# Local-attention and whitening kernel: the first image prepared as a whole, the row point at infinity by column points in images 2 and 3, interpolations one bank later

## The chip, the cores and the metric

The kernel runs on one NeuronCore of a Trainium2 chip, with everything in float32. The metric is device microseconds (us) of one launch. A core has five engines with a queue each: TensorE (PE, matmuls and transposes through the array; its weight loads are shown apart as PEld), VectorE (DVE), ScalarE (ACT), GpSimd (POOL) and SyncE (SP, which here only issues DMAs). Each engine takes its own instructions in order and waits on semaphores for the others.

## The reference, cut to what matters

```python
k = lax.conv_general_dilated(x, w1, padding=[(6, 6), (6, 6)], rhs_dilation=(2, 2), ...) + b1   # 7x7, 256 -> 128 channels
k = lax.conv_general_dilated(k, w2, ...) + b2                                                   # 1x1, 128 -> 49
attn = jax.nn.softmax(k, axis=1)
shifts = jnp.stack([xp[:, :, 2*u:2*u+64, 2*v:2*v+64] for u in range(7) for v in range(7)], axis=1)
y = jnp.einsum('bkchw,bkhw->bchw', shifts, attn)
# then, over all images: 4 groups of 64 channels, covariance Sigma, five Newton steps P = 1.5 P - 0.5 P^3 Sigma_N, and wm (y - mean)
```

The input x has 4 images (numbered 0 to 3 here) of 256 channels by 64 by 64 pixels.

## The kernel before, in words

**Layout.** The two convolutions are multiplied into one, 256 to 49 channels, 7 by 7 taps. A dilation of 2 splits an image into even and odd rows, and each of these into even and odd columns. One half of the rows goes to output partitions 0 to 48, the other to 64 to 112, so a result tile has 113 partitions.

**The convolution by points.** Along each axis the sum of 7 taps is a product of polynomials, and both factors are evaluated at seven points: 0, 1, -1, 2, -2, 1/2 and infinity (`INF`, number 6). A *row point* is handled in these steps. `row_eval` (L423) evaluates x along the rows into one of three tiles `rb`. `col_eval` (L454) evaluates that along the columns into seven tiles `xh`, in three *banks*: points (1, 2, 0), (3, 4, 6) and (5). `weights` (L355) makes, the first time that a row point is met, the weights of a bank by the same kind of sums, and stores them in DRAM (`gd`); later images load them from there. `conv_bank` (L482) multiplies a bank on TensorE into one of two PSUM tiles `cv`, and ScalarE copies it to `pv`. When the three banks are done, `col_interp` (L556) interpolates the seven column points back to columns, and writes row `br` of the tile `zz`. When all row points of an image are there, `row_interp` (L569) interpolates along the rows and gives the logits. Both call `interpolate` (L517), a chain of 22 VectorE operations that is written out in an order by hand, on elements of 113x162 (columns) or 113x576 (rows). Its work tile is `it`, a piece of the tile `ct`, for columns (`ct` is also the scratch of `col_eval` and `weights`), and a tile of its own, `zi`, for rows.

**Direct rows.** A row point can also be convolved without column points, with the 7 column taps as they stand (`direct`, L594: 28 products of up to 512 columns). Image 0 does row points 1, 2, 3 by column points and INF, 0, 4, 5 directly; images 1 to 3 do 0 to 5 by column points and INF directly (`direct_inf`, L632).

**Image 0** (L698 to L756) is a list written by hand, and `in_turn` (L277) makes VectorE keep exactly that order. In it, the interpolation of row 1 stands between the preparations of rows 3 and 5, and that of row 2 behind row 5.

**Images 1 to 3** run as 18 *steps* each, `conv_step` (L655) for six row points by three banks: multiply a bank; prepare the same bank of the next row point in the same tiles (`xh` and the weight tiles have one buffer); after the third bank, interpolate. The last two row points are interpolated `in_order` (L292), at high priority. Between the steps lie *gaps*, set by costs (6, 5, 2 for the banks of a row, 12 for the direct row; L1146 to L1164): gap j of an image comes when (j+1)/8 of the cost is done. Into the gaps `plan` (L1109) has put the softmax of the image before (`soft`), and the attention: `first_half` and `second_half` of four pixel classes n per image. These load bands of attention weights from DRAM (`band`), turn them by VectorE transposes (`load_band`, L890), transpose x and multiply (`weighted_sum`), transpose the result and add up the moments. TensorE keeps the program's order; the other engines' queues are ordered by a planner, by priority and its own costs.

**Loads.** GpSimd's queue fetches images 1 to 3; image 2's and 3's halves go into space that the attention of an earlier image must have left (`move`, L1021). SP's queue has all the other DMAs, each waiting its turn.

After image 3's convolution the remaining attention runs alone (about 605 to 695 us), then whitening, then the application to all pixels (to 765 us).

Of the kernel before, what the change touches and what calls it, by code (L numbers as in the profile page):

```python
# [27 lines left out]
ROWS = (0, 1, 2, 3, 4, 5)  # L28
# [3 lines left out]
def kernel(  # L32
# [222 lines left out]
    zz = apool.tile([P, NP - 1, Q9, W], F32, name="zz")  # L255
    zi = [apool.tile([P, Q9, W], F32, name=f"zi{k}") for k in range(2)]
    for k in range(2):
        nc.gpsimd.memset(zi[k], 0.0)
    ct = apool.tile([P, Q8 * 4 * Q8, 4], F32, name="ct")
    it = ct.rearrange("p a b -> p (a b)")[:, :PT].rearrange("p (q b) -> p q b", q=Q9)  # L260
# [10 lines left out]
    gd = [dram.tile([P, nsl, NSK], F32, name=f"gd{b}") for b in range(NP - 1)]  # L271
# [42 lines left out]

    def keep_weights(br):
        f = (gb5 if br == 5 else gbr).rearrange("p v a r k -> p (v a r k)")
        nc.scalar.mul(f, f, SCALE[br])
        nc.sync.dma_start(kept[br], f)

    def row_weights(br):  # L320
# [8 lines left out]
        if br == 1:  # L329
            add(E, T[6], T[4])  # L330
            add(O, T[5], T[3])
            add(S0, E, O)
            add(E1, T[2], T[0])
# [4 lines left out]
        elif br == 3:  # L338
            madd(E, T[4], 4.0, T[6])
            madd(O, T[3], 4.0, T[5])  # L340
            madd(S0, O, 2.0, E)
            madd(E1, T[0], 4.0, T[2])
            madd(S1, T[1], 2.0, E1)
        elif br == 4:
            madd(S0, O, -2.0, E)
            madd(S1, T[1], -2.0, E1)
        else:
            madd(S0, T[6], 2.0, T[5])
            madd(S0, S0, 2.0, T[4])
            madd(S0, S0, 2.0, T[3])  # L350
            madd(S1, T[2], 4.0, T[0])
            madd(S1, T[1], 2.0, S1)
            add(S1, S1, S1)

    def weights(b, br, i):  # L355
# [9 lines left out]
        wt = apool.tile([P, ns, NSK], F32, tag=f"wr{i}", name=f"wr_{b}_{br}_{i}")  # L365
# [7 lines left out]
        elif br in kept:  # L373

            f = rb[0].rearrange("p q r c w -> p (q r c w)")[:, : KS * NSK]
            if i == 0:
                nc.sync.dma_start(f, kept[br])
            f = f.rearrange("p (v a r k) -> p v a r k", v=KS, a=NCC, r=2)
            g = [f[:, v] for v in range(KS)]
        else:  # L380
            g = [gbr[:, v] for v in range(KS)]
        g = [t.rearrange("p a r k -> p (a r k)") for t in g]
        e, o, e1 = (
            ct.rearrange("p a b -> p (a b)")[:, k * NSK : (k + 1) * NSK] for k in range(3)
        )
# [4 lines left out]
        if i == 0:  # L390
            add(e, g0[0], g0[2])
            add(o, g0[1], g0[3])
            add(o0[1], e, o)
            sub(o0[2], e, o)
            add(e1, g1[0], g1[2])
# [4 lines left out]
        elif i == 1:  # L400
            madd(e, g0[2], 4.0, g0[0])
            madd(o, g0[3], 4.0, g0[1])
            madd(o0[3], o, 2.0, e)
            madd(o0[4], o, -2.0, e)
            madd(e1, g1[2], 4.0, g1[0])
# [3 lines left out]
        else:  # L409
            madd(o0[5], g0[0], 2.0, g0[1])  # L410
            madd(o0[5], o0[5], 2.0, g0[2])
            madd(o0[5], o0[5], 2.0, g0[3])
            madd(o1[5], g1[0], 4.0, g1[2])
            madd(o1[5], g1[1], 2.0, o1[5])
# [8 lines left out]
    def row_eval(b, br, rb=rb):  # L423

        for pr in range(2):
# [5 lines left out]
            elif br == 0:  # L431
                nc.scalar.copy(r[2], xs[:, 0])
            for cc in range(NCC):
                X = [xs[:, a, :, cc] for a in range(4)]
                q = [t[:, :, cc] for t in r]
                if br == 3:
                    madd(q[1], X[2], 4.0, X[0])
                    madd(q[2], X[3], 4.0, X[1])
                elif br == 5:
                    madd(q[2], X[0], 2.0, X[1])  # L440
                    madd(q[2], q[2], 2.0, X[2])
                    madd(q[2], q[2], 2.0, X[3])
# [9 lines left out]
        return rb[{1: 2, 2: 0, 3: 0, 4: 1, 5: 2, 0: 2}[br]]  # L452

    def col_eval(src, i):  # L454
# [9 lines left out]
        if i == 0:  # L464
            add(EO, X[:, :, 0:2], X[:, :, 2:4])
            add(o[1], E, O)
            sub(o[2], E, O)
            nc.scalar.copy(o[0], X4[0])
        elif i == 1:
            madd(EO, X[:, :, 2:4], 4.0, X[:, :, 0:2])  # L470
            madd(o[3], O, 2.0, E)
            madd(o[4], O, -2.0, E)
            nc.scalar.copy(o[INF], X4[3])
        else:
            madd(o[5], X4[0], 2.0, X4[1])
            madd(o[5], o[5], 2.0, X4[2])
            madd(o[5], o[5], 2.0, X4[3])

    ncv = [0]
    pvs = {}  # L480

    def conv_bank(b, br, i, w):  # L482

        if i == 0:
            pvs[b, br] = apool.tile(
                [P, NP, Q9, 2 * Q9], F32, tag="pv", name=f"pv_{b}_{br}", bufs=2
            )
# [23 lines left out]
        with tc.high_priority():  # L511
            nc.scalar.copy(  # L512
                pvs[b, br][:K2, i0 : i0 + len(pts)].rearrange("p n q b -> p (n q b)"),
                cv[:K2, : len(pts)].rearrange("p n q b two -> p (n q b two)"),
            )

    def interpolate(pt, tmp, outs, cut, part=None):  # L517

# [8 lines left out]
        if part != 1:  # L527
# [4 lines left out]
            add(s3, c0, c6)  # L532
            sub(s3, tmp, s3)
            madd(s1, tmp, -2.0, s1)
            madd(tmp, tmp, -30.5, s1)
            madd(tmp, s3, 22.5, tmp)
            madd(s1, c0, 1.5, s1)
            madd(s1, c6, -30.0, s1)
            madd(s3, s1, -1.0 / 6, s3)
            sub(s4, s4, s2)  # L540
            madd(tmp, s2, -16.0, tmp)
            add(tmp, tmp, s4)
            madd(outs[0], lo(s1), 1.0 / 6, hi(c0))
            add(outs[2], lo(c6), hi(s3))
        if part != 0:
            madd(hh, tmp, -1.0 / 9, hh)
# [5 lines left out]
    def phases(t):  # L552

        return [t[:, :, bass.ds(4 + a - R if a < R else 0, Q8, 4)] for a in range(4)]

    def col_interp(b, br, part=None):  # L556
        pv = pvs[b, br]
        pt = {c: pv[:K2, i] for i, c in enumerate(ORDER)}
        outs = phases(zz[:K2, br].rearrange("p q (w two) -> p q w two", two=2))
        cut = lambda t, k: t[:, :, 2 * k : 2 * (k + Q8)].rearrange("p q (b two) -> p q b two", two=2)  # L560
        t = it
        if part is not None:

            t = pvs[b, ROWS[-2]][:, 0]
        interpolate(pt, t[:K2], outs, cut, part)
# [818 lines left out]
```

## Time and profile before

| | |
|---|---|
| median of 3 runs | 761.5 us (761.24 to 763.82) |
| the profiled execution: its time | 767.1 us |
| its span, first to last instruction | 765.3 us |
| PE busy, of the span | 710.7 us, 93% |
| DVE busy | 630.3 us, 82% |
| ACT busy | 332.4 us, 43% |
| image 0's convolution | to about 171 us |
| images 1, 2, 3 (from one direct row to the next) | about 171 to 301, 301 to 453, 453 to 605 us |

How to read it: busy time is the union of an engine's instructions. A matmul's end is modelled, so a busy PE isn't PE at its peak; and consecutive VectorE instructions overlap in the records, so what one costs is read from the distance between two starts, not from its own duration. Times in the text count from the span's start.

### The profile page before, as it was taken

The page shows a single profiled execution, that of the slowest core. Times are in us where ns is not written, and L with a number is a line of the kernel's source. Part 1 is how long each engine was busy: PE and PEld are TensorE (multiplying, and loading weights), DVE is VectorE, ACT ScalarE, POOL GpSimd, SP SyncE. Part 2 cuts the span into 40 slices and gives each one's busy share as a digit, 9 for nine tenths or more (in the row PEclk, how much of TensorE's full clock was granted, in tenths as well). Part 3 has the DMA queues.
Part 4 walks back from the last instruction along what each step waited for, and adds up shares of the span by engine and source line. Part 5 has one row for each costly group of instructions (what it writes and reads, how often), then busy time and mean ns, then how long its engine had stood idle before and what let it go on. Part 6 is the DMA issues. An engine that isn't in the chain of part 4 may idle for free.

```text
span 765.3 us, 18542 instructions
## 1 busy us (share of the span) xinstructions
PE 710.7 (93%) x7512; PEld 538.0 (70%) x7512; DVE 630.3 (82%) x1312; ACT 332.4 (43%) x958; POOL 34.4 (4%) x48
## 2 busy tenths in 40 slices
PE   6989899969899999989999999999999889998996
PEld 1449564365798887779988967798898768885322
DVE  3769999999899999989996899699979775645565
ACT  2413241025555454366444443635435473322464
POOL 0410000020000010001000100000000000000000
PEclk9999999979999999999999999999999999999999
DMA  8991110042654393056734920533532233362487
GB/s 323 238 322 65 39 75 38 1 155 68 200 153 156 122 351 91 20 160 205 235 120 141 313 70 1 155 90 110 166 88 80 49 115 128 115 251 111 190 362 327
DMA packets 59773, 114.76 MB, mean 150 GB/s; under 512 B 22903, under 2 KB 42024, under 8 KB 58920
## 3 DMA queue, kind: packets, MB, share of 16 engines
q1 hardware_dynamic: 55992, 94.71, 37.5%
q0 software_dynamic: 3696, 18.88, 7.2%
q8 instruction: 59, 0.97, 0.5%
q14 instruction: 26, 0.21, 0.1%
HBM read 66.23 MB, written 47.33 MB: 148 GB/s over the span
## 4 chain that ended last, share of the span: by engine, by line
DVE 43%; PE 32%; ACT 5%; issue 5%; DMA 2%; SPq 0%; DVEq 0%; ACTq 0%
PE y L955 10%; PE cv L502 7%; DVE xh L307 5%; PE tp L1324 4%; DVE rb L307 3%; DVE pv L307 3%; DVE zz L307 3%; DVE ct L307 3%; DVE ct L300 3%; DVE band L908 3%; PE sig L1008 3%; PE tp L987 2%; PE tp L926 2%; DVE pv L303 2%; DVE rb L300 2%
## 5 line engine op out<-in xcount | busy, mean ns | idle before, releaser
L502 PE MATMUL cv<-xh,wr 128*49 128x128 f32 x4368 | 253.7, 278 | 14.3 <-DVE xh L300 11.5
L502 PEld LDWEIGHTS cv<-xh,wr 128*49 128x49 f32 x4368 | 247.3, 125 | 19.9 <-issue 12.9
L955 PE MATMUL y<-band,xb 128*128 128x224 f32 (+2 forms) x640 | 153.4, 379 | 12.5 <-ACT xb L934 8.3
L955 PEld LDWEIGHTS y<-band,xb 128*128 128x128 f32 x640 | 111.2, 196 | 34.4 <-ACT xb L934 10.8
L974 ACT ACTIVATE slot<-y,pivot 128x512 f32<-128x512 f32 x53 | 36.7, 740 | 60.0 <-PE y L955 60.0
L512 ACT COPY pv<-cv 113x486 f32<-113x486 f32 (+1 forms) x63 | 29.8, 474 | 74.9 <-PE cv L502 73.7
L995 ACT COPY yt<-tp 128x256 f32<-128x256 f32 x128 | 45.5, 379 | 34.8 <-PE tp L987 33.8
L926 PE MATMUL tp<-ident,slot 128*128 128x128 f32 x256 | 50.3, 299 | 7.1 <-ACT yt L995 7.1
L987 PE MATMUL tp<-ident,slot 128*128 128x128 f32 x256 | 52.0, 299 | 4.0 <-ACT xb L934 1.4
L908 DVE STREAM_TRANSPOSE band<-band 128x960 f32<-128x960 f32 (+1 forms) x48 | 50.8, 1059 | 4.9 <-DMA band<-sd 4.8
L987 PEld LDWEIGHTS tp<-ident,slot 128*128 128x128 f32 x256 | 41.3, 205 | 13.9 <-issue 4.5
L926 PEld LDWEIGHTS tp<-ident,slot 128*128 128x128 f32 x256 | 40.0, 206 | 14.4 <-ACT yt L995 9.0
L857 ACT COPY zt<-d 32x112 f32<-32x112 f32 (+2 forms) x156 | 45.0, 288 | 1.7
L811 ACT ACTIVATE d<-tp,mx 128x49 f32<-128x49 f32 x128 | 37.0, 336 | 15.1 <-DVE mx L806 15.1
L307 DVE SCALAR_TENSOR_TENSOR xh<-ct 128x512 f32<-128x512 f32 x42 | 27.7, 681 | 12.2 <-PE cv L502 12.0
L934 ACT COPY xb<-tp 128x256 f32<-128x256 f32 x87 | 30.4, 376 | 15.8 <-PE tp L926 15.2
L1008 PE MATMUL sig<-yt 128*64 128x65 f32 x1024 | 36.9, 225 | 0.0
L1008 PEld LDWEIGHTS sig<-yt 128*64 128x64 f32 x1024 | 32.5, 138 | 6.0 <-issue 4.4
L608 PE MATMUL cv<-slot,wi 128*49 128x496 f32 (+3 forms) x168 | 34.8, 571 | 0.0
L934 DVE COPY xb<-tp 128x256 f32<-128x256 f32 x41 | 16.4, 421 | 22.2 <-PE tp L926 22.2
L307 DVE SCALAR_TENSOR_TENSOR pv<-pv 113x162 f32<-113x162 f32 x105 | 33.5, 319 | 1.0
L419 ACT ACTIVATE wr<-wr 128x392 f32<-128x392 f32 (+1 forms) x36 | 17.3, 512 | 31.1 <-DVE wr L300 18.8
(224 smaller groups left out, 999.9 us busy)
## 6 DMA issues: line engine op xcount, KB each, us to landing
out_dram<-out SPq DMA_DIRECT2D x32, 512.0 KB, 3.4
sd<-zt SPq DMA_DIRECT2D x16, 896.0 KB, 3.9
slot<-in_x_dram POOLq DMA_DIRECT2D x12, 1024.0 KB, 9.6
band<-sd SPq DMA_DIRECT2D x128, 84.0 KB, 2.1
wr<-gd SPq DMA_DIRECT2D x15, 588.0 KB, 3.8
wr<-gd SPq DMA_DIRECT2D x15, 490.0 KB, 3.6
spill<-slot POOLq DMA_DIRECT2D x3, 2048.0 KB, 8.4
back<-spill SPq DMA_DIRECT2D x3, 2048.0 KB, 7.7
```

The lines of the kernel that those rows point to most:

```text
L300: return in_turn(TT(o, a, b, ALU.add))
L307: return in_turn(STT(o, a, f, b, ALU.mult, ALU.add))
L502: nc.tensor.matmul(cv[h * HB : h * HB + KT, k, sr : sr + n, sc : sc + n], wv[:, sc, sr, cc], xh[bc][:, :n, h * NCC + cc, :n], start=(j == ...
L811: nc.scalar.activation(d[:, h, i], lt[i // NI][:, i % NI, h, :KT], AF.Exp, bias=mx[:, i, h : h + 1], accum_out=s[:, h, i : i + 1],)
L857: ins = nc.scalar.copy(o, i)
L908: nc.vector.transpose(f, f)
L926: nc.tensor.transpose(t[:, cc * P : (cc + 1) * P], xt[:, cc, CR * m : CR * (m + 1), bass.ds(pc, SW, 2)], ident,)
L934: (nc.vector.tensor_copy if tail else nc.scalar.copy)(xb, t[:, :C])
L955: nc.tensor.matmul(ps[:, cc, q0 - half * HALF : q1 - half * HALF, :], xb[:, cc * P : (cc + 1) * P], rhs, start=(k == 0), stop=(k == len(PI ...
L987: nc.tensor.transpose(t[:, cc * P : (cc + 1) * P], yt[:, cc, CR * i : CR * (i + 1), bass.ds(pc, SW, 2)], ident,)
L995: nc.scalar.copy(yb.rearrange("p a g c -> p (a g) c")[:, :, :GW], t[:, :C].rearrange("p (e c) -> p e c", c=GW),)
L1008: nc.tensor.matmul(sig[g * GW : (g + 1) * GW, cc], yb[:, cc, g, :GW], yb[:, cc, g], start=(count[0] == 0 and cc == 0), stop=(count[0] == 4 ...
```

## The change

It has these parts.

- **Order of operations.** In `interpolate`, `weights`, `row_weights` and `row_eval` the same VectorE operations come in another order, in which fewer of them touch what the one just before them wrote or read. For image 0, `both0` deals the operations of `weights` and `col_eval` of a bank out alternately (so `weights` has its scratch in slot 4 there, not in `ct`); `col_ops` is `col_eval` as a generator that pauses behind its first operation.
- **Image 0's list.** All rows are evaluated and multiplied first, and the three column interpolations come behind `row_eval(0, 5)`.
- **INF by column points.** `ROWS` begins with INF. Images 2 and 3 have seven row points and no direct row. Image 1's direct INF is done at the end of image 0's list, with the taps that still lie in SBUF, and not in its steps. INF's weights are made in image 2 (half as long as the others, 98 elements) and loaded in image 3. `zz` gets a seventh row; `zi` and the tile `wi` are gone.
- **Interpolation one bank later.** A row's `col_interp` is issued behind the preparation that follows the *next* row's first bank. `pv` has three slots, not two, and `col_interp`'s work tile is a piece of a `pv` slot, not of `ct`; `row_interp`'s is now in `ct`. ScalarE's last copy of an interpolation is ordered behind the next second bank (`later`).
- **Steps and gaps.** Softmax (0, 0) comes before image 1's first bank and softmax (0, 1) behind its third. INF's steps cost half, so that the gaps shift against the rows: in image 1 gap 2 comes behind row 2's first bank (before: row 1's second), gap 5 behind row 4's second (before: its first); in images 2 and 3 gap 0 comes behind row 0's first bank, with INF's three banks ahead of it.
- **First transposes.** For n = 0 the three band transposes are kept in a list, `held`, and ordered behind the last operation of softmax (0, 1).

```diff
-ROWS = (0, 1, 2, 3, 4, 5)
+ROWS = (INF, 0, 1, 2, 3, 4, 5)
...
+    NV = 3
+    pv = apool.tile([P, NV, NP, Q9, 2 * Q9], F32, name="pv")
...
+    kept[INF] = dram.tile([P, KS * NSK // 2], F32, name="gi")
+    nc.sync.dma_start(kept[INF], tap[:, UPOS[3]].rearrange("p v a k -> p (v a k)"))
...
@@ weights @@
         if i == 0:
             add(e, g0[0], g0[2])
             add(o, g0[1], g0[3])
+            add(e1, g1[0], g1[2])
             add(o0[1], e, o)
             sub(o0[2], e, o)
-            add(e1, g1[0], g1[2])
...
             madd(o0[5], g0[0], 2.0, g0[1])
+            madd(o1[5], g1[0], 4.0, g1[2])
             madd(o0[5], o0[5], 2.0, g0[2])
+            if mid is not None:
+                mid()
+            madd(o1[5], g1[1], 2.0, o1[5])
             madd(o0[5], o0[5], 2.0, g0[3])
-            madd(o1[5], g1[0], 4.0, g1[2])
-            madd(o1[5], g1[1], 2.0, o1[5])
             add(o1[5], o1[5], o1[5])
...
+    def both0(src, br, i):
+        g = col_ops(src, i)
+        next(g)
+        nxt.update(weights(0, br, i, lambda: next(g)))
+        for _ in g:
+            pass
...
@@ interpolate @@
             add(s3, c0, c6)
+            madd(s1, tmp, -2.0, s1)
             sub(s3, tmp, s3)
-            madd(s1, tmp, -2.0, s1)
             madd(tmp, tmp, -30.5, s1)
+            sub(s4, s4, s2)
             madd(tmp, s3, 22.5, tmp)
             madd(s1, c0, 1.5, s1)
+            madd(tmp, s2, -16.0, tmp)
             madd(s1, c6, -30.0, s1)
+            if part is None:
+                add(tmp, tmp, s4)
             madd(s3, s1, -1.0 / 6, s3)
-            sub(s4, s4, s2)
-            madd(tmp, s2, -16.0, tmp)
-            add(tmp, tmp, s4)
...
@@ col_interp @@
-        t = it
+        if b > 0:
+            t = pv[:K2, (at + 2) % NV, NP - 1].rearrange("p q b -> p (q b)")
+        else:
+            t = ct.rearrange("p a b -> p (a b)")[:K2, :PT]
...
@@ row_interp @@
-        tr = zi[(b + 1) % 2]
+        tr = ct.rearrange("p a b -> p (a b)")[:K2, : Q9 * W].rearrange("p (q w) -> p q w", w=W)
...
@@ conv_step @@
         if k + 1 < len(rows):
             prepare(k + 1, i)
+        if waiting:
+            col_interp(*waiting.pop())
         if i == len(BANKS) - 1 and not end:
-            if b > 0 and br == ROWS[-2]:
+            if br != ROWS[-2]:
+                waiting.append((b, br))
+            else:
                 with in_order():
                     col_interp(b, br)
                     row_interp(b, 0)
-            else:
-                col_interp(b, br)
...
@@ image 0's list, its end @@
     row_eval(0, 5, [rb[0], rb[1], xrs[5]])
+    col_interp(0, 1)
     col_interp(0, 2)
     direct0(4, 1)
+    direct0(5, 0)
     col_interp(0, 3)
     row_interp(0, 0)
-    direct0(5, 0)
-    for i in three:
-        prepare(NR0, i)
+    prepare(NR0, 0)
     direct0(5, 1)
     row_interp(0, 1)
+    direct(1, INF, 0, acc[:, 0], [tap[:, UPOS[3], v] for v in range(KS)])
+    prepare(NR0, 1)
+    prepare(NR0, 2)
...
@@ load_band @@
+        if n == 0:
+            held.append(turn_blocks)
+        else:
+            turn_blocks()
...
+                    steps.append(
+                        (cost * len(taps(br)) / 2, lambda k=k, i=i: conv_step(k, i))
+                    )
         if b == 1:
-            steps[:3] = [
-                *steps[:3], (0, lambda: soft(0, 0)), inf, (0, lambda: soft(0, 1)),
-            ]
-        else:
-            steps.insert(0, inf)
+            steps.insert(0, (0, lambda: soft(0, 0)))
+            steps.insert(4, (0, lambda: soft(0, 1)))
```

## The prediction, made before the changed kernel was run

> **What bounds the kernel now.** I read the page first: engine shares and the chain that ended last.
>
> ```profile
> span 765.3 us, 18542 instructions
> ...
> PE 710.7 (93%) x7512; PEld 538.0 (70%) x7512; DVE 630.3 (82%) x1312; ACT 332.4 (43%) x958; POOL 34.4 (4%) x48
> ...
> DVE 43%; PE 32%; ACT 5%; issue 5%; DMA 2%; SPq 0%; DVEq 0%; ACTq 0%
> ```
>
> PE and DVE are both nearly full, and the chain changes between them, so no single total decides. I then cut the span at the direct rows and asked for busy times by stretch (columns: us, then PE, PEld, DVE, ACT, POOL busy, clock, DMA):
>
> ```profile
> 58.00:171.26 113.26, 100.92 (x967) 65.03 (x965) 108.77 (x218) 29.72 (x61) 6.73 (x8) 0.94 0.17 63
> 171.26:300.80 129.54, 123.36 (x1560) 106.03 (x1556) 124.81 (x273) 68.45 (x219) 5.63 (x4) 0.98 0.52 167
> 300.80:453.45 152.65, 146.95 (x1866) 127.30 (x1865) 136.00 (x281) 75.25 (x234) 8.03 (x7) 0.99 0.50 159
> 453.45:605.00 151.55, 145.48 (x1828) 126.24 (x1828) 136.47 (x282) 70.75 (x227) 1.14 (x7) 0.99 0.31 93
> 605.00:695.00 90.00, 84.40 (x771) 70.20 (x769) 47.28 (x102) 40.04 (x144) 0.00 (x0) 1.00 0.46 157
> ```
>
> Image 0 (58 to 171) is DVE: 108.8 of 113.3 us, with PE waiting. Image 1 is DVE: 124.8 of 129.5. Images 2 and 3 are PE first (147.0 of 152.7; 145.5 of 151.6), with DVE at 136. The last row, attention alone, is PE.
>
> Busy hides stalls, so I read the DVE timeline. This is column interpolation in image 0's fixed order (columns: start, own time):
>
> ```profile
> 104.23 0.32 DVE L300 TENSOR_TENSOR ct<-pv 113x162 f32<-113x162 f32 x1
> 104.58 0.33 DVE L303 TENSOR_TENSOR pv<-pv 113x162 f32<-113x162 f32 x1
> 104.94 0.33 DVE L300 TENSOR_TENSOR pv<-pv 113x162 f32<-113x162 f32 x1
> ```
>
> The starts are 0.35 to 0.36 us apart. The same kind of operation in image 1, where the planner deals two strands out alternately:
>
> ```profile
> 192.01 0.32 DVE L303 TENSOR_TENSOR pv<-pv 113x162 f32<-113x162 f32 x1
> 192.25 0.32 DVE L307 SCALAR_TENSOR_TENSOR pv<-ct,pv 113x162 f32<-113x162 f32 x1
> 192.49 0.32 DVE L300 TENSOR_TENSOR pv<-pv 113x162 f32<-113x162 f32 x1
> ```
>
> Here they are 0.24 apart. An operation that reads or overwrites what the one before it used costs some 0.12 us more. Over the stretch 58 to 171 I took, for each DVE operation, the distance to the next start less that of the independent case (162 elements 0.24, 196 0.28, 512 0.60, 576 0.68, 686 0.79, 1024 1.14, 2048 2.20): 98.5 us of need and 13.7 of stalls. Images 2 and 3: need 130 each, stalls 7, true idle 15.5. DVE needs 123 of image 1's 129.5.
>
> [...]
>
> **The change, part by part.**
>
> *1. Image 0's order.* Adjacent pairs that touch the same data, counted in the source: an interpolation goes from 13 to 7, three of them, 18 fewer; row interpolation 3; `weights` 8 per row, for three rows (row 1's are made before x has landed at 46.9 us, so worth nothing), 24; dealing out `weights` and `col_eval` for rows 2 and 3, 8, and row 1's, 3; `row_weights` 6; `row_eval` of row 5, 8. That is 70, times 0.12 us = 8.4 of the 13.7. Moving the interpolations behind `row_eval` of row 5 costs DVE nothing and gives PE its inputs sooner. PE then has three direct rows in a line, 11.5 us each, and image 1's INF. By my list DVE reaches the addition of direct row 5's second half at about 150 us and PE at about 149, so an us may be lost to PE. I take -7.0; bounds -10 and -3 (PE late).
>
> *2. Image 1.* Its direct INF, 11.5 us of PE, goes to where DVE works on the last row interpolation and on row 0's banks 1 and 2 (9 us behind it). DVE bounds image 1, so this alone gives nothing. One DVE wait goes, on the first band's DMAs:
>
> ```profile
> 201.35 1.18 DVE L908 STREAM_TRANSPOSE band<-band 128x960 f32<-128x960 f32 x1 [2.79 <-DMA band<-sd]
> ```
>
> The held transposes let 2.8 us of other work pass. In exchange, attention starts a bank later against the rows, and PE has more of it to do in the second half. -2.0; bounds -5 and +2.
>
> *3. INF by column points, images 2 and 3.* PE, a row of two taps and a direct row:
>
> ```profile
> 343.62 11.80 PE L502 MATMUL cv<-xh,wr 128*49 128x128 f32 x208
> 453.45 11.59 PE L608 MATMUL cv<-slot,wi 128*49 128x512 f32 x56
> ```
>
> 208 records in 11.73 us (to the next start) are 104 products at 0.113. INF has 52 products: 5.9 us against 11.5, so -5.65 per image. DVE gets more: `col_eval` two operations on 1024 (1.14) and seven on 512 (0.60), 6.5; an interpolation of 22, 5.2; in image 2 20 weight operations on 98 elements, [...] 3.6. So +15.3 in image 2 and +11.7 in image 3. ACT gets two copies of 1.05, two of 0.68, one of 0.34, and in image 2 three copies and five scalings, some 2 us: 4 to 6 of its 75, and it has half its time free. DMA: one load of 343 KB (the same as the `wi` loads that it replaces, 4.6 us), three stores, three loads, in rows of 392 bytes; under 4 us each by the loads of 490 KB (3.6). They stand in SP's queue behind band loads, which wait for ScalarE; INF's land while the row interpolation below still runs. POOL gets a small memset that waits for INF's interpolation, ahead of the next spill (342.7 us before), which feeds a load needed only some 80 us later: nothing.
>
> Where DVE's extra lies decides. The image's end before:
>
> ```profile
> 298.91 0.68 DVE L300 TENSOR_TENSOR lgx<-zi,zz 113x512 f32<-113x512 f32 x1
> 299.51 0.32 DVE L300 TENSOR_TENSOR pv<-pv 113x162 f32<-113x162 f32 x1
> 299.75 1.22 DVE L300 TENSOR_TENSOR ct<-rb 128x1024 f32<-128x1024 f32 x1
> ```
>
> A strand at high priority, the last interpolations, ends at 299.5; only then does the next image's first `ct` come, though its `rb` was copied by 289. PE was covered meanwhile by the direct row, which needs nothing of DVE. Now INF does: 6.5 + 3.6, and row 0's first bank 2.4 more, 12.5 us in image 2 and 8.9 in image 3, mixed with up to 12.7 of the strand's rest (col_interp 5.2, a row part 3.7, transposes 2.8, stalls 1). The cover is what PE has left when the strand's first part ends: in image 2 1.3 us, plus 5.5 because gap 5 now stands between the strand's beginning and the bank that it waits for, about 7; in image 3 6.3 + 1; and INF's own 5.9 of PE. So 13 us cover against 12.5 (all INF first) to 25 (strand first): PE waits 0 to 12, midway 6; in image 3 0 to 9, midway 4.5. Against -5.65 that is +0.4 and -1.2. INF's interpolation, 5.2, goes into the 15.5 of idle later, since `ct` no longer ties it to `col_eval` and there are three `pv` slots; 1 us of friction each. Image 2 +1.4 (bounds -6, +8), image 3 -0.2 (-6, +6). `later` only orders a copy of 0.34 us.
>
> *4. Image 3's end.* Its last interpolations are on the chain to 602 us; fewer pairs (6+3) by 0.12: -0.7. Attention alone, whitening and application don't change.
>
> Sum: -7.0 - 2.0 + 1.4 - 0.2 - 0.7 = -8.5. The profiled execution is 767.1 us (span 765.3 and 1.8 around it), 5.6 above the median of 761.5; on it, 758.6; on the median, **753.0**.
>
> **Rivals.**
>
> *DVE fills up (faster yet).* With `ct` untied and interpolations deferred, DVE's 15 us of idle per image take all that is added, and PE's relief counts whole: -5 in both images, -20 at most with part 1 whole: 741 to 748. For it: DVE need in image 2 is then 145, PE 137, both under 152. Against it: the idle lies in mid-image (9.4 us of it between 382 and 421), the new work at the start.
>
> *The gain is eaten.* PE is late in image 0 (-3), part 2 and 4 give their 2.7, the junctions cost +1 to +4 each: 757.8 to 763.8, taken as 757.7 to 765.3.
>
> *Slower: the junctions become DVE's.* INF is prepared behind the whole strand, PE waits 12 to 16 us at each, and the softmax transposes and attention behind it on PE wait too; ScalarE's evictions then come in a heap with the exponentials (PE already waits 6 us there at 331 to 343). Two waits of w, each less 5.65 and plus 1 of friction, against -9.7 from parts 1, 2 and 4: at w = 11.4 the kernel is 0.5% slower, the point that decides; at 14 it is 770.5. So 765.5 to 771. For it: the chain before runs through DVE from 283 to 330 and from 447 to 480.
>
> *It doesn't do what it says.* If the planner already separates touching pairs, order gains nothing; in image 0 it cannot, as the order is fixed.
>
> **How the numbers follow.** No change measurable is within 0.5%: 757.7 to 765.3. Chances: forecast (748 to 757.7) 0.42, faster yet 0.19, eaten 0.21, slower 0.18. So faster 0.61, same 0.21, slower 0.18. Leaving out the ends of the outer cases, 0.2 in all: 741 to 768. The forecast's own range is 748 to 757.7.
>
> **What would show it.** Image 0's DVE timeline has starts 0.24 apart in most of an interpolation, and the row interpolation ends near 155, the list near 163 us. Image 1 ends near 290. At both junctions PE's first INF bank waits for DVE `xh` or `wr`; its records are 104. DVE busy in images 2 and 3 rises to about 148. Wrong if: PE gaps in image 0 above 11 us; PE waits of 10 us and more per junction; or image 2 longer than 158.

## The result, and the profile after

The changed kernel takes 765.9 us (median of 20 runs, 763.05 to 772.75), the kernel before 761.5 (20 runs, 756.27 to 764.05). The ratio is 1.007, with a 95% interval of 1.0051 to 1.0088: 0.7% slower (0.6% by the medians alone), where I had forecast 753.0 and faster. An execution more than 1.5% above the fastest of its kernel counts as slow; medians and ratios are of the others. The profiled execution of the kernel after took 764.03 us. Its page:

```profile
PE 700.2 (92%) x7608; PEld 539.2 (71%) x7608; DVE 642.6 (84%) x1394; ACT 342.7 (45%) x980; POOL 33.7 (4%) x45
...
PE 55%; DVE 34%; ACT 5%; issue 3%; DMA 2%; SPq 0%; DVEq 0%; ACTq 0%
```

PE has 10.5 us less than before and DVE 12.3 more: infinity's work moved as the diff says (the runs below put that at 23.3 us more for DVE), and the new order of operations saves DVE some 11 (630.4 before, 619.2 with image 0's part alone). The chain that ended last runs less through DVE (34% after 43%) and more through PE, and still the kernel is slower.

**The trace of before was no typical one.** The two profiled executions stand 3 us apart in favour of the kernel after (767.1 and 764.0), the medians 4.4 against it. A second profile of the kernel before has a span of 759.9 and took 761.6 in the median. DVE's timeline where image 0's x arrives, first in the execution on record (start, own time, and the wait ahead in brackets):

```profile
46.91 2.36 DVE L300 TENSOR_TENSOR rb<-slot 128x1024 f32<-128x1024 f32 x2 [6.47 <-DMA slot<-in_x_dram]
```

The same in the second execution, all four operations in one line:

```profile
38.22 4.62 DVE L300 TENSOR_TENSOR rb<-slot 128x1024 f32<-128x1024 f32 x4
```

In the first, half of x landed 6.5 us later; the next operation starts late by that (49.30 against 42.87 us), and 5.4 us of it are left in the span (765.3 against 759.9). From here on the second execution stands for the kernel before. Busy times of images 1, 2 and 3 (us, then PE, PEld, DVE, ACT, POOL busy, clock, DMA share, GB/s), cut about where image 0's list ends (before) or where PE begins row 0 of image 1 (after), at the heads of images 2 and 3, and where image 3's softmax begins; the kernel before, second execution:

```profile
164.50:294.49 129.99, 122.32 (x1546) 104.99 (x1542) 125.39 (x273) 68.36 (x219) 5.63 (x4) 0.99 0.52 166
294.49:449.33 154.84, 148.96 (x1865) 128.52 (x1864) 137.65 (x287) 75.14 (x234) 8.03 (x7) 0.98 0.48 156
449.33:600.63 151.30, 145.84 (x1865) 126.89 (x1865) 135.72 (x278) 71.44 (x228) 1.14 (x7) 1.00 0.31 93
```

The kernel after:

```profile
157.97:294.96 136.99, 121.62 (x1629) 111.42 (x1628) 132.18 (x304) 72.00 (x229) 9.65 (x10) 0.96 0.49 155
294.96:447.86 152.90, 142.93 (x1913) 130.69 (x1912) 140.07 (x303) 79.05 (x241) 8.03 (x7) 0.98 0.53 163
447.86:603.29 155.43, 142.41 (x1914) 130.35 (x1914) 146.08 (x315) 73.75 (x233) 0.99 (x6) 0.98 0.34 99
```

The first cut isn't the same place in both: before, PE has most of image 1's row 0 behind it there, after, image 1's direct row. Image 0's gain shows where both are done: PE's last transposes of softmax (0, 1), behind row 0 and the direct row, first before, then after:

```profile
180.57 1.21 PE L797 MATMUL tp<-ident,slot 113*128 113x113 f32 x8
```

```profile
169.70 1.21 PE L850 MATMUL tp<-ident,slot 113*128 113x113 f32 x8
```

Image 0 is won: PE is 10.9 us ahead there, and DVE's list ends at 158.92 where it ended at 165.05. But the head of image 2 stands where it stood (294.96 against 294.49), image 2 gains 1.9, and image 3 loses 4.1. In images 2 and 3 PE is busy 6.0 and 3.4 us less, and little or nothing of it comes through in the time.

What happens at the junctions, where one image ends and the next begins, shows at the head of image 3 in three views of the kernel after. PE's timeline:

```profile
451.29 2.68 PE L531 MATMUL cv<-xh,wr 128*49 128x128 f32 x40 [0.56 <-DVE xh L310]
461.32 8.27 PE L531 MATMUL cv<-xh,wr 128*49 128x128 f32 x112 [7.34 <-issue]
```

DVE's timeline over that wait:

```profile
453.93 1.55 DVE L310 SCALAR_TENSOR_TENSOR zz<-zz 113x576 f32<-113x576 f32 x2
...
457.59 0.68 DVE L310 SCALAR_TENSOR_TENSOR xh<-rb 128x512 f32<-128x512 f32 x1
...
460.53 0.68 DVE L310 SCALAR_TENSOR_TENSOR xh<-xh,rb 128x512 f32<-128x512 f32 x1
```

And the granted clock, in stretches of 2 us (columns as above):

```profile
460.00:462.00 2.00, 0.68 (x8) 0.71 (x10) 2.00 (x5) 0.00 (x0) 0.00 (x0) 0.50 0.00 0
462.00:464.00 2.00, 2.00 (x22) 2.00 (x20) 2.00 (x2) 0.29 (x1) 0.00 (x0) 0.50 0.00 0
464.00:466.00 2.00, 2.00 (x30) 2.00 (x28) 2.00 (x5) 0.00 (x0) 0.00 (x0) 0.70 0.38 100
466.00:468.00 2.00, 2.00 (x42) 2.00 (x38) 2.00 (x3) 0.00 (x0) 0.00 (x0) 1.00 0.03 8
```

PE stops at 454.0, with infinity's third bank still to come. DVE has work all the while: it does the row interpolation of image 2, then the three `xh` operations of that bank, and PE goes on when the last of them is done (460.53 + 0.68 = 461.21). The page calls the wait "issue", because it finds no semaphore event for it. Behind it PE runs at half clock for 4 us, which costs 2 more. The first trace of the kernel before has the same in image 0, in PE's timeline and in stretches of 2 us:

```profile
157.53 7.43 PE L502 MATMUL cv<-xh,wr 128*49 128x128 f32 x96 [5.58 <-DVE xh L300]
```

```profile
156.00:158.00 2.00, 0.47 (x6) 0.51 (x8) 1.95 (x3) 0.20 (x2) 2.00 (x5) 0.50 0.55 219
158.00:160.00 2.00, 2.00 (x22) 2.00 (x20) 1.92 (x7) 0.00 (x0) 0.64 (x1) 0.50 0.45 117
160.00:162.00 2.00, 2.00 (x26) 2.00 (x24) 1.93 (x3) 0.95 (x2) 0.00 (x0) 0.62 1.02 346
```

These 96 records take 7.43 us; at the rate of 208 in 11.73 they would take 5.41, so 2.0 are lost. In the kernel after, at the head of image 2 the wait stands ahead of infinity's second bank:

```profile
303.11 4.62 PE L531 MATMUL cv<-xh,wr 128*49 128x128 f32 x40 [5.27 <-DVE xh L310]
```

Infinity and row 0's first bank, 200 records, took 19.43 us in image 2 and 21.65 in image 3; at the rate of row 0 alone (208 records in 11.73) they take 11.28. So PE lost 8.2 and 10.4 us at the junctions, half-speed stretches included. I had taken 6 and 4.5.

The slow clock has a large share in this. An estimate: the span times what the mean granted clock lacks of 1 is 19.6 us in the 20 executions of the kernel after, and 13.4 to 15.8 in five groups of executions of the kernel before. Not all of that falls where PE is the bound, so it is an upper limit; but the difference, 4 to 6 us, is as large as the whole loss.

### The profile page after: what moved, and what is told of

The parts are those of the page before. It is cut to its first block, busy times and chain, and to the rows that moved or that the text cites. A ratio compares the mean times of both kernels' runs of the same rounds, so it can differ in the third digit from the quotient of the medians.

```text
span 762.3 us, 18839 instructions
## 1 busy us (share of the span) xinstructions
PE 700.2 (92%) x7608; PEld 539.2 (71%) x7608; DVE 642.6 (84%) x1394; ACT 342.7 (45%) x980; POOL 33.7 (4%) x45
## 4 chain that ended last, share of the span: by engine, by line
PE 55%; DVE 34%; ACT 5%; issue 3%; DMA 2%; SPq 0%; DVEq 0%; ACTq 0%
PE cv L531 17%; PE y L1028 11%; PE acc L668 6%; PE tp L1396 4%; DVE xh L310 4%; DVE pv L310 3%; PE tp L1060 3%; PE sig L1081 3%; DVE zz L310 3%; PE tp L999 3%; DVE ct L310 3%; DVE rb L310 2%; DVE band L976 2%; PE cv L222 2%; DVE ct L303 2%
## 5 line engine op out<-in xcount | busy, mean ns | idle before, releaser
L531 PE MATMUL cv<-xh,wr 128*49 128x128 f32 (+1 forms) x4576 | 267.5, 278 | 20.1 <-issue 7.3
L531 PEld LDWEIGHTS cv<-xh,wr 128*49 128x49 f32 x4576 | 259.1, 125 | 26.3 <-issue 18.7
L541 ACT COPY pv<-cv 113x486 f32<-113x486 f32 (+1 forms) x69 | 33.0, 480 | 94.5 <-PE cv L531 94.3
L310 DVE SCALAR_TENSOR_TENSOR pv<-pv 113x162 f32<-113x162 f32 x215 | 64.4, 318 | 0.8 <-ACT pv L541 0.2
L310 DVE SCALAR_TENSOR_TENSOR xh<-ct 128x512 f32<-128x512 f32 x46 | 30.6, 685 | 9.3 <-PE cv L531 9.3
L306 DVE TENSOR_TENSOR pv<-pv 113x162 f32<-113x162 f32 x112 | 34.9, 321 | 0.4
L668 PE MATMUL acc<-slot,tap 128*49 128x496 f32 (+3 forms) x168 | 34.6, 569 | 0.0
## 6 DMA issues: line engine op xcount, KB each, us to landing
back<-spill SPq DMA_DIRECT2D x3, 2048.0 KB, 12.8
```

Of the source, the lines that this page charges most:

```text
L310: return in_turn(STT(o, a, f, b, ALU.mult, ALU.add))
L531: nc.tensor.matmul(cv[h * HB : h * HB + KT, k, sr : sr + n, sc : sc + n], wv[:, sc, sr, cc], xh[bc][:, :n, h * NCC + cc, :n], start=(j == ...
L668: nc.tensor.matmul(ps[h * HB : h * HB + KT, :, w0:w1_], w[v][:, cc], xs[:, :, cc, w0 + d : w1_ + d], start=(j == 0), stop=(j == len(order) ...
```

## Experiments

Each is named by its edit of the kernel after, unless said otherwise. Ratios are to the kernel before on the same chip, whose median was 760.8 to 762.0; the text compares medians across these chips as they are. In short:

| run | median us | ratio, 95% interval |
|---|---|---|
| kernel after | 765.9 | 1.007 (1.0051 to 1.0088) |
| kernel before again | 761.6 | 0.9993 (0.9977 to 1.0009) |
| infinity direct | 756.8 | 0.9936 (0.9913 to 0.9958) |
| interpolations at once | 761.2 | 0.9996 (0.998 to 1.0013) |
| image 0 alone | 755.3 | 0.9926 (0.9903 to 0.995) |
| infinity direct, at once | 752.6 | 0.9879 (0.985 to 0.9909) |
| the same, transposes not held | 753.1 | 0.9889 (0.9854 to 0.9924) |
| the same, other buffers | 753.7 | 0.9884 (0.9852 to 0.9916) |
| direct row in mid-image | 761.6 | 1.0006 (0.9986 to 1.0026) |
| column points in mid-image | 758.1 | 0.9968 (0.9946 to 0.999) |
| image 0 alone, old succession | 767.3 | 1.0076 (1.0042 to 1.011) |
| cover back | 772.2 | 1.0119 (1.0079 to 1.0159) |
| copy free | 765.6 | 1.0067 (1.0042 to 1.0093) |
| inputs first | 766.6 | 1.0098 (1.007 to 1.0127) |
| infinity direct, inputs first | 755.6 | 0.9944 (0.9929 to 0.9959) |
| deferred in images 2, 3 alone | 765.0 | 1.0066 (1.0035 to 1.0097) |

**The kernel before again** (no edit).

> The kernel before once more, for its profile. The profiled execution on record (767.1 us) lies above all its timed runs. If that execution was an odd one, a new profile reads near 762, and the 4 to 6 us less lie in one or two stretches that can be named. If every profiled execution of this kernel is slow, it reads 767 again.

761.6 us in the median, span 759.9: the first trace was the odd one, and its 5.4 us more come from one wait, shown above.

**Infinity direct in images 2 and 3.**

```diff
-    rows += [(b, br) for b in range(1, B) for br in ROWS[1 if b == 1 else 0 :]]
+    rows += [(b, br) for b in range(1, B) for br in ROWS[1 if b in (1, 2, 3) else 0 :]]
...
+        elif b in (2, 3):
+            steps.insert(0, (12, lambda b=b: direct_inf(b)))
```

> The kernel after with part 3 undone: in images 2 and 3 infinity is again one direct row of PE, with its weights loaded into a row buffer that is free then; images 0 and 1, the deferred interpolations and the held transposes stay. Theory J (the column points of infinity load VectorE at the junctions, where PE then waits 8 to 11 us, and this eats what image 0 won): well below the kernel after and below the kernel before, 753 to 758 us, images 2 and 3 each 2 to 4 us shorter than the kernel after. Theory D (deferring the interpolation by a bank, or the new order in image 1, loses the gain): 764 to 768, as the kernel after. In the traces the images 2 and 3 of before and after are nearly equal in length, which speaks for D; the medians are not explained by the traces, which leaves room for J.

756.8: 9 us below the kernel after and 5 below the kernel before, as theory J had it. The edit also moves the gaps, whose places follow from the costs of the steps: gap 0 of images 2 and 3 now comes right behind the direct row, and not behind row 0's first bank.

**Interpolations at once.**

```diff
-        if waiting:
-            col_interp(*waiting.pop())
...
-                waiting.append((b, br))
+                col_interp(b, br)
```

> The kernel after with every interpolation dealt out at once, behind its row's last bank, as before, and with its last copy not held back; all else as after. If deferring by a bank is what costs (theory D), it is 3 to 6 us faster than the kernel after: 760 to 763. If it makes no odds, 765 to 767. If deferring helps (an interpolation no longer stands ahead of the next bank's inputs on VectorE), it is slower, 768 or more.

761.2: deferring costs 4.7 us. So theory D holds too, beside J.

**Image 0 alone.** Both edits above, and infinity of image 1 back among the steps, and the transposes not held.

> Of the change only image 0's order, the reordered operations and the third set of point buffers: infinity direct in images 1, 2 and 3 (in image 1 at its old place among the steps), interpolations at once, transposes not held. My step 1 says -7.0 us against the kernel before: 754 to 757. The trace of the kernel after shows image 0's list 12 us earlier: then 750 or so. If a gain in image 0 is given back in image 1 whatever stands there (since the attention behind it waits for something else), 759 to 763.

755.3, 6.5 below the kernel before beside it (761.9): step 1's size.

**Infinity direct at the head, interpolations at once** (the first two edits together).

> From the kernel after, infinity direct at the head of images 2 and 3 (weights loaded into a row buffer free there) and interpolations dealt out at once, three sets of point buffers as in the kernel after; image 0's order, image 1's early infinity and the held transposes stay. Against the same with the interpolations deferred (756.8 us) it shows what deferring costs where infinity is direct: 753 to 754 if some 3 us, 756 to 757 if nothing. It should beat both kernels.

752.6, a ratio of 0.9879: 1.2% faster than the kernel before and the best of all. Deferring costs 4.2 us here as well, so it isn't tied to the column points. Its image 2:

```profile
294.26:440.61 146.35, 145.02 (x1865) 126.46 (x1864) 126.41 (x258) 74.73 (x232) 7.87 (x6) 1.00 0.52 165
```

Image 0's gain does not show at the head of image 2 here either (294.26). It shows as work that DVE has behind it by then (126.4 us are left to it in image 2, 137.7 in the kernel before), and image 2 is 8.5 us shorter, with PE busy for 145 of 146 us. The kernel after spends this lead on infinity. PE at the head of image 3:

```profile
440.61 11.59 PE L666 MATMUL cv<-slot,rb 128*49 128x512 f32 x56
...
460.77 10.02 PE L531 MATMUL cv<-xh,wr 128*49 128x128 f32 x176
```

Between the direct row and row 0 lies gap 0, 8.6 us of attention and transposes without a wait. So PE has 20 us to do here before it needs row 0's inputs. What column points at the head would cost if gap 0 stayed ahead of them was not run; this rival, that the gap's place makes a part of the 8.6 us between this run and interpolations at once, is open.

One more stretch of this run, for the clock. PE waits 1.01 us up to 473.90 and 0.61 us up to 475.29, so for 1.6 of the 2.4 us from 472.89; half clock follows:

```profile
476.00:478.00 2.00, 2.00 (x6) 1.34 (x5) 1.59 (x7) 0.00 (x0) 0.00 (x0) 0.57 0.71 266
```

**The same with two sets of point buffers and a tile of infinity's own**; image 0's third row then writes its points where the first row's still stand, so image 0's logits come out different, with the same operations in the same shapes. It is the base of the direct row in mid-image, below.

> From the kernel after, both suspects undone: infinity direct at the head of images 2 and 3 (weights in a tile of their own, two sets of point buffers), interpolations dealt out at once. Left of the change: image 0's order, image 1's infinity early on the weights that are still there, the held transposes. Against image 0 alone (755.3 us) it tells what my step 2 is worth: step 2 as forecast (-2.0) gives 753 to 754; worth nothing, 755 to 756; if the early row and the held transposes cost, 757 or more. Against the same with the interpolations deferred (756.8) it tells what deferring costs where infinity is direct: 3 to 5 us if it costs as much as with the column points, else 0 to 2.

753.7.

**The transposes not held** (in the best one).

```diff
-        if n == 0:
-            held.append(turn_blocks)
-        else:
-            turn_blocks()
+        turn_blocks()
```

> The last kernel with the first image's band transposes no longer held behind the second softmax. My step 2 put the wait that holding them removes at 2.8 us and the whole of image 1 at -2.0: 1.5 to 3 us above the last kernel if that is so; within 1 us if VectorE only waits elsewhere.

753.1, 0.5 more, with overlapping intervals: not told apart from nothing.

**Direct row in mid-image**, from the one with the other buffers (its image 0 as there).

```diff
-            steps.insert(0, (12, lambda b=b: direct_inf(b)))
+            steps.insert(9, (12, lambda b=b: direct_inf(b)))
+            steps.insert(1, (0, lambda b=b: load_inf(b)))
```

> The last kernel with infinity's direct row moved in images 2 and 3 from the head of the image to behind row 2, its weights loaded ahead; VectorE has the same work as there. Theory C (the cover: what counts is that at the junction PE has 11.5 us of work that needs nothing of VectorE): PE waits 6 to 10 us at each junction for row 0's inputs, runs slow behind that, and the time is 6 to 10 us above the last kernel, 760 to 765. Theory L (the load: the 12 to 15 us more of VectorE per image cost, wherever they stand): within 1.5 us of the last kernel.

761.6: 7.9 us for moving a row that costs DVE nothing. PE at the head of image 3:

```profile
445.92 10.03 PE L532 MATMUL cv<-xh,wr 128*49 128x128 f32 x176
460.12 3.66 PE L532 MATMUL cv<-xh,wr 128*49 128x128 f32 x32 [4.18 <-issue]
```

Without the direct row PE waits there even for row 0's inputs, those of its third bank, and the 32 records behind the wait take nearly twice their time. But theory C had such a wait at both junctions, and at the head of image 2 there is none:

```profile
304.83 1.98 PE L532 MATMUL cv<-xh,wr 128*49 128x128 f32 x32 [0.25 <-issue]
```

Image 2 is 5.0 us longer all the same (151.4 against 146.4): PE waits 2.5 us for ScalarE's `xb` at 351 us, shortly ahead of the moved row, and runs slow behind that too (clock 0.62 and 0.53 in the next 4 us). So the time is as theory C had it, and its mechanism shows at one head of two; the moved gaps (gap 0 now comes behind row 0's third bank) are not taken apart from it.

**Column points in mid-image**, interpolations at once.

```diff
+            for br in (ROWS[1:] if b == 1 else (0, 1, 2, INF, 3, 4, 5))
```

> Infinity by column points in images 2 and 3 but as the fourth row, behind row 2, where VectorE has its idle time; interpolations at once, image 0 and 1 as in the kernel after. The same with infinity first: 761.2 us. Theory C (cover): the junctions have no direct row, so PE waits for row 0's inputs, which are 4 us fewer than infinity's; the gain over infinity first is only that, 757 to 760. Theory L (load): VectorE's total is the same, 760 to 763. If only infinity's place was wrong (its 10 us of VectorE at the junction), PE's 5.65 per image come through and it is 750 to 755.

758.1, 3.1 below infinity first (761.2) and 3.5 below the direct row in mid-image: in the middle the column points do win, at the head they lose 8.6 (761.2 against 752.6). The heads of both images have no wait now, though no direct row stands there (176 records in 9.95 us at each). In this run gap 0 falls behind row 0's second bank, and its attention keeps PE busy while DVE makes the third bank's inputs: attention is cover too. PE waits for `xh` behind infinity instead, 4.8 us in image 2 and 3.4 in image 3:

```profile
375.41 11.98 PE L531 MATMUL cv<-xh,wr 128*49 128x128 f32 x176 [4.80 <-DVE xh L303]
```

So even there only 3.5 of the 11.3 saved come through, and the place of the gaps is a part of this comparison.

**Cover back**: 56 products in the shapes of the direct row at the head of images 2 and 3, with the identity as weights; nothing reads the sums. The computation is otherwise that of the kernel after, and the step's cost is set to 0, so that the gaps stay where they are.

```diff
+        else:
+            steps.insert(0, (0, lambda b=b: cover(b)))
```

> The kernel after (infinity by column points first in images 2 and 3) with 11.5 us of PE put back at the head of these images: 56 products in the shapes of the direct row, whose sums nothing reads and nothing waits for. It gives PE two times 11.5 us more to do and nothing else. Theory C (at the junction PE would only wait): of the 23 us most is free, 766 to 772 us, and the waits of 6 to 8 us and the slow clock behind them are gone. If PE's work there counts fully, 785 to 789.

772.2, 6.3 above the kernel after for 23 us of PE. PE at the head of image 3:

```profile
458.13 11.59 PE L699 MATMUL cv<-slot,ident 128*49 128x512 f32 x56
469.55 5.99 PE L531 MATMUL cv<-xh,wr 128*49 128x128 f32 x104
476.73 5.53 PE L531 MATMUL cv<-xh,wr 128*49 128x128 f32 x96 [1.19 <-DVE rb L303]
```

The wait of 7.3 us is 1.2, and infinity's 104 records run without a break at full clock; at the head of image 2 a wait of 0.7 is left. Of the 8.2 and 10.4 us that PE lost there in the kernel after, 0.8 and 1.3 remain. So 16.5 us come back, and that is what the added work didn't cost: 23 less 6.3 is 16.7. This is the clean test of theory C.

**Image 0 alone with the old succession of operations**: `interpolate`, `weights`, `row_weights`, `row_eval` of row 5 and the dealing out of rows 1 to 3 as before; for example

```diff
-            madd(s1, tmp, -2.0, s1)
             sub(s3, tmp, s3)
+            madd(s1, tmp, -2.0, s1)
```

> Image 0's list alone (755.3 us) with the operations inside it back in their old succession: the interpolations, the weights, the row weights, the row evaluation of row 5, and the dealing out of rows 1 to 3; the list's larger pieces stay in the new succession. My step 1 counted 67 of these touching pairs at 0.12 us, of which some 60 lie on the path: 762 to 763, the kernel before's time. If the gain came from the larger pieces (PE gets its inputs sooner), 755 to 757.

767.3: the succession is worth 12.0 us, more than the 7 to 8 expected. But `interpolate` and `weights` serve all images, so the edit reaches past image 0. Its interpolation in image 0, to set against the kernel after's:

```profile
120.08 0.33 DVE L306 TENSOR_TENSOR pv<-pv 113x162 f32<-113x162 f32 x1
120.45 0.33 DVE L303 TENSOR_TENSOR pv<-pv 113x162 f32<-113x162 f32 x1
```

The kernel after, further down in one:

```profile
113.61 0.32 DVE L310 SCALAR_TENSOR_TENSOR pv<-pv 113x162 f32<-113x162 f32 x1
113.85 0.32 DVE L310 SCALAR_TENSOR_TENSOR ct<-pv,ct 113x162 f32<-113x162 f32 x1
```

The starts are 0.37 and 0.24 apart. By the traces PE is done with image 1's row 0, its direct row and the softmax at 181.80 with the old succession and at 176.31 with the new: 5.5 us lie in image 0, of which 2.9 are left at the head of image 2 (304.07 against 301.16). Image 2 adds 2.8 (149.3 against 146.5), and image 3 with the last softmaxes 3.6. The last 3.4 of the 12.8 us between these two traces lie behind the last softmax, where both run the same program, with 10.2 us of half clock in one and 3.4 in the other.

**Copy free**: the deferred interpolation's last copy no longer ordered behind the next row's second bank.

```diff
-        if part is None and b > 0 and br != ROWS[-2]:
-            later.append(end)
-        elif part != 0:
+        if part != 0:
```

> The kernel after with the interpolations still deferred by a bank, but their last copy on ScalarE no longer ordered behind the next row's second bank. Dealing everything out at once was 4.7 us faster than the kernel after (761.2 against 765.9). If the copy's order is what costs, this reads 761 to 762 too; if the deferral itself does, 765 to 767.

765.6, as the kernel after (765.9): the order of the copy is not what costs.

These give the sizes; the next ones ask for the cause.

**Inputs first**, with interpolations at once.

```diff
             with in_order():
+                if k + 1 < len(rows):
+                    prepare(k + 1, i)
                 if i == len(BANKS) - 2:
...
-        if k + 1 < len(rows):
+        elif k + 1 < len(rows):
```

> Infinity by column points first in images 2 and 3, interpolations at once (761.2 us), and on VectorE the next image's first inputs put in front of the last interpolations of the image (each bank's weights and points first, then the interpolation of the bank before). If the succession on VectorE makes TensorE's waits at the junction (my step 3's end 'strand first' against 'infinity first'), these fall from 8 to 10 us to under 4 and the time to 753 to 757. If the amount of VectorE's work does, the wait only changes its place (the last logits, the softmax and the attention come later): 760 to 764.

766.6, 5.4 more, above what either reading had. PE at the head of image 2:

```profile
293.51 5.15 PE L531 MATMUL cv<-xh,wr 128*49 128x128 f32 x88
303.54 1.95 PE L531 MATMUL cv<-xh,wr 128*49 128x128 f32 x16 [4.88 <-DVE xh L310]
311.17 7.06 PE L531 MATMUL cv<-xh,wr 128*49 128x128 f32 x96 [5.67 <-DVE xh L303]
```

Infinity's first two banks now run without a break; the wait stands ahead of the third and of row 0. The succession only moves it: DVE has too much to do there.

**The same succession where infinity is direct.**

> The same change of succession where infinity is a direct row (752.6 us): row 0's first inputs in front of the last interpolations. The direct row covers these inputs either way, so the succession should give nothing: 751 to 755; above that, the delayed logits cost by themselves.

755.6, 3.0 above the best one: with row 0's inputs covered either way, this is put down to the later logits, so the strand at high priority, the last interpolations of an image, is rightly in front.

**Deferred in images 2 and 3 alone.**

> The kernel after with the interpolations deferred by a bank in images 2 and 3 alone, at once in image 1. All at once: 761.2, all deferred: 765.9. If image 1, where VectorE is the bound and waits at row 5's weights once the interpolation is not there to fill, has the cost: 761 to 762.5. If it lies in images 2 and 3: 764.5 to 766.

765.0: the cost of deferring is in images 2 and 3. By the traces image 2 is 155.3 us long, against 152.0 with all at once: PE falls behind by 0.8 us up to 333 us, by 1.7 at 352, and by less elsewhere, with no one cause that I can show. Infinity's stretch at image 3's head takes 22.6 against 20.9, with the same wait in it (7.35 us in both): 15.3 us are outside the wait against 13.6. Half clock has a part in the medians too: by the estimate used above it takes 19.6 us in the kernel after and 17.0 with all at once, 14.1 and 12.5 where infinity is direct.

## Why the prediction was wrong

By its steps, with the medians (kernel before 761.5):

- **Step 1, -7.0: right.** Image 0 alone gives -6.5; DVE's list ends 6.1 us earlier; the stalls of DVE between 76 and 176 us, by the distances that I gave, fall from some 12 to some 5 us. The mechanism is shown too: with the old succession all of the gain goes. But what I costed at nothing, the move of the list's larger pieces, may not be free: with the old succession the kernel is 5.3 slower than the kernel before beside it (762.0). That run also has the new buffers, and its image 0 is no later than the kernel before's (181.80 against 181.71 us at the same place), so what costs isn't settled. PE late behind the direct rows showed once, 3.6 us ahead of the addition of direct row 0's second half (86.69 us), not where I looked for it.
- **Step 2, -2.0: right in size, wrong in place.** The best one is 2.7 below image 0 alone, the one with other buffers 1.7; the intervals of the ratios just touch. That the held transposes have a part in it is not shown (0.5 with overlapping intervals). "Image 1 ends near 290" was wrong: 294.3 in the best one. The lead is handed on as DVE work done and comes out as time in image 2.
- **Step 3, +1.2: this failed**, as +8.6 (761.2 against 752.6). Its PE term was right: 10.8 us less busy (695.5 against 706.3) where I had 11.3. Its DVE term was near: 23.3 more busy (642.2 against 618.9), and I had 27; the 20 weight operations on 98 elements, put at 3.6 us by an estimate of mine (the distances that I gave for 162 and 196 elements, 0.24 and 0.28, lead to 3.3), last some 0.25 us each in the kernel after and start 0.17 apart where they follow one another (303.49, 303.66, 303.83 us), so 3.4 in all. The failing step is "PE waits 0 to 12, midway 6; in image 3 0 to 9, midway 4.5". In the kernel after PE lost 8.2 and 10.4 at these places, with interpolations at once 7.8 and 9.6. With the latter in the sum, -11.3 + 17.5 + 2 of friction (as assumed) is 8.2, near the 8.6 measured. Midway was wrong three times over. I set infinity's own 5.9 us of PE against all of DVE's work, as cover, though its banks need that work first: the waits stand ahead of infinity's second bank in image 2 and its third in image 3. I took the order on DVE as open between two ends, where inputs first shows that neither end is cheap. And half clock behind each of the two waits lost some 2 to 2.5 us, which I hadn't costed (by the granted clock it lasts 3.9 us from PE's restart at 461.32, and 5.1 from that at 303.11). The first trace of the kernel before shows it, as above: 2.0 us lost behind a wait of 5.58; so the price of a long wait was to be had ahead of the run. Nor does it take one long wait (the stretch at 476 us of the best one, above: waits of 1.01 and 0.61 us, then a clock of 0.57). The sum also hid what the direct row was: 11.5 us of PE that nobody could have used, since PE was not the bound at that place. Cover back says the same from the other side. How much of the 8.6 the gaps have, which also moved, is open.
- **Deferring, costed at nothing: this failed**, as +4.7. I wrote that infinity's interpolation goes into DVE's idle time later and that `later` only orders a copy. The second half holds (copy free), but all interpolations a bank later cost 4 to 5 us, with column points (4.7) and without (4.2), and with column points the cost lies in images 2 and 3 (765.0). What makes it is open; more half clock is some 2 us of it, by the estimate above.
- **Step 4, -0.7: not settled.** The 3.6 us above have the right sign and are more, but they cover all of image 3 and come from one pair of executions.

Together: -8.9 for steps 1, 2 and 4, where I had -9.7; +8.6 and +4.7 where I had +1.2 and nothing: +4.4. Of my signs of failure none was met: the longest wait was 7.3 us (10.4 are lost at that junction, but only with the slow stretch behind it), and PE's gaps and image 2's length stayed below their marks. The rival "slower" had the right place and, with 765.5 to 771, the time; its point of decision (11.4 us per junction) was not reached, and the deferral, which it didn't have, made up the rest; so its range came true in part by luck. The rival "faster" had PE at 137 us in image 2; 147.0 less 5.65 is 141, and 142.9 was measured. Taking the profiled execution's excess of 5.6 us as a constant offset was harmless for the sum; but I had read image 0's stretch from an execution with a late load in front of it.

## What to carry to other kernels

Before taking PE work away, ask which engine is the last to finish at that place. A long piece of PE work that needs nothing of DVE is cover: while DVE is behind, taking it away wins nothing, and a slow clock behind the new wait is lost on top (some 2 us behind the one of 7.3). Other work that is ready, here attention, can be the cover if it is placed there. The same exchange of PE for DVE work lost 8.6 us at the head of an image and won 3.5 in its middle (the gaps moved with it in both). And where DVE is in front of the chain, set independent operations between dependent ones first: 12 us of 767 from the succession alone.

## What the runs showed of the hardware

- PE, though busy for 92% of the kernel after, ran slow behind each wait of 4.2 us or more that the views of the runs above show (4.2 to 7.3): 32 records took 3.66 us behind the one of 4.18 and 176 took 11.98 behind the one of 4.80, where the rate of row 0 gives 1.80 and 9.93; some 2 us were lost behind the longest. In the kernel after, behind a wait of 3.38 us for ScalarE's `xb` that ends at 277.18 us, eight products of 224 columns for `y` take 2.42 us, at 617.14 us eight take 1.34; the clock from 278 to 280 us is 0.50. Behind the single wait of 1.2 us of cover back nothing of that shows; behind the one of 2.5 us in the direct row in mid-image it does (as above), and behind two short ones close together, shown above, too.
- Behind the last softmax the edits change nothing, yet this stretch took 143.7 to 147.3 us in the profiled executions: 143.7 to 143.9 where the clock was halved once for 3.4 us in it before its last few us, and 145.5 to 147.3 where it was so for 6.8 or 10.2. Two traces can so differ by 3 us there.
- The same load of x landed 6.5 us later in one execution than in another, and the span was 5.4 us longer: one profiled execution can be off by more than the effect one looks for.
- DVE operations of 162 elements, 0.32 us long, start 0.24 apart or 0.36 apart, as they leave alone or touch what the one before used. In image 0 DVE's stalls fell by some 7 us for the 70 such pairs that the prediction counted, about 0.1 us each.
